# Two sequence layers on one core: the Hadamard transform of W2 moved from TensorE to VectorE and GpSimd, head states in 32 columns, first loads on three queues

## The chip, the core and the metric

One core of a Trainium2 chip runs one program. The metric is the device time of one execution in microseconds (us), as the median of several runs. The engines are TensorE (PE; its weight loads are listed as PEld), VectorE (DVE), ScalarE (ACT), GpSimd (POOL) and SyncE (SP, which here only issues DMAs). All arithmetic is float32.

## What is computed

Two layers act on 2 sequences of 1024 tokens with 512 features; each layer is a mixing part and a feed-forward part, each followed by an addition and a layer norm.

```
layer 0: x = norm(x + lightning_attention(x))      16 heads of 32, chunks of 128 tokens,
                                                   a state of 32x32 per head, decayed per chunk
         x = norm(x + fwht(silu(x W1) * (x W3)) W2) hidden size 2048, fwht = Hadamard / sqrt(2048)
layer 1: x = norm(x + selective_scan(x))           512 channels x 32 states, one step per token
         x = norm(x + (silu(x Wg) * (x Wu)) Wd)    hidden size 2048
```

The Hadamard transform acts on the hidden vector, and the matrix is symmetric. So `fwht(h) W2` equals `h (H W2) / sqrt(2048)`: the kernel transforms the 2048 rows of W2 once and keeps the result `w2h` in HBM, instead of transforming every token.

## The kernel before, in words

**Order of the work.** The kernel has a list scheduler of its own (class `Order`). Each operation is an `Op` with an engine, an estimated duration, the buffers that it reads and writes, and a priority. `Order.run` takes, again and again, the operation that can begin first by these estimates (then the lower priority number), and so writes out one fixed order for each engine. On the chip each engine works through its list in that order and waits where an operand isn't ready. The estimates (`mm_us`, `dve`, `act`, `pool`, `dma` and single numbers in the code) therefore decide the order, and nothing else. `dma` estimates a queue of its own of 220 GB/s for each issuing engine.

**Groups and phases.** The 2048 tokens are five groups of 2, 4, 4, 4 and 2 chunks of 128 tokens. Group g passes the phases V (values of the attention), A (attention), F (feed-forward of layer 0), then the scan of layer 1, then f (feed-forward of layer 1; for groups 1 and 2 the f of the group before runs in halves, a and b). The phases of later groups and the f phases fill PE while DVE, ACT and POOL work on a scan.

**Weights.** `load_weights` brings 256 KB pieces through a ring of 12 buffers, in the order of use, all on SP's queue. The pieces of the second matrix of F come from `w2h` and wait until all of it is stored.

**First loads** (`load_first`): on SP the identity, x of group 0 (2 chunks), one constant, x of group 1 (4 chunks), then Wv, two quarters of W2, Wq, Wk, two more quarters of W2, and the small constants.

**W2** (`transformed_w2`, `butterflies` L1152, `w2_products` L1171): four quarters of 128 of its 512 columns. In a quarter, row 128 c + p lies in partition p at place c (tile 128 x 16 x 128). DVE does the 4 butterfly steps over c (two operations of 1024 columns each, two tiles `w2f` and `w2b` taking turns). PE multiplies by a 128 x 128 Hadamard matrix (4 products of 512 columns a quarter) for the steps over p, ACT scales by 1/sqrt(2048) from PSUM (L1178), and SP stores the quarter.

**Attention blocks** (`attention`, `block`): a block has four heads (128 features) and four slots of 128 tokens. PE transposes the keys (L717), DVE multiplies by key decays (`kd`, L724), PE forms the state updates, one 128x128 product for each chunk (L780) of which only the four 32x32 diagonal blocks are wanted; DVE masks them with `blk` (L788) and chains them over the chunks (L796, L798) into `own` and `last`. PE forms scores (L828), DVE multiplies them by the decay mask (L846), PE adds the state's part (L872, 128x128) and the scores' part (L880) in one bank, DVE gates (L899), and a norm over each head follows (PE L916, ACT, DVE L931). Decayed queries `qd` are made by DVE for group 0, by POOL for the others (L736).

**Scan** (class `Scan`): for each of 32 states POOL multiplies `du` by B (L1375), ACT makes exp(delta a) (L1395), DVE scans (L1423) and multiplies by C (L1436), POOL (L1472) and an accumulating DMA on POOL's queue sum the products. The tile `da` of the scans lies in PSUM; `dbu`, `du`, B and C lie in SBUF. The softplus of `delta` ends with an addition of two SBUF tiles on DVE (L1307). PE transposes the sums `y` (L1501).

Of the kernel before, what the change touches and what calls it, by code (L numbers as in the profile page):

```python
# [16 lines left out]
P = 128  # L17
# [184 lines left out]
def two_layers(  # L202
# [25 lines left out]
    Pools = type("Pools", (), {"sb": None, "w2": 0, "w": 0})  # L228
# [14 lines left out]
    tagged("own", 2, lambda: wk1, [P, CG - 1, P])  # L243
    tagged("last", 3, lambda: ap_, [P, EB, P])
# [4 lines left out]
    tagged("w2f", 4, lambda: tw, [P, FC, D // 4])  # L249
    tagged("w2b", 3, lambda: tw, [P, FC, D // 4])  # L250
# [18 lines left out]
    def mm_us(n, cols):  # L269
        return n * max(cols * 4 / 2400 + 0.006, 0.28 if cols <= P else 0)  # L270
# [4 lines left out]
    def dve(cols, fn, **kw):  # L275
        return Op("DVE", 0.145 + cols * 1.05e-3, fn, **kw)
# [4 lines left out]
    def pool(cols, fn, **kw):  # L281
        return Op("POOL", 0.15 + cols * 2.25e-3, fn, **kw)
# [12 lines left out]
    w2h_b = [Buf() for _ in range(4)]  # L295
# [50 lines left out]
    def load_weights():  # L346
        for i, (src, b, needs) in enumerate(pieces):
            if i in (EB, 3 * EB):
                Pools.w = i
                yield lambda: Pools.w2 >= i // EB // 3 * 2 + 2  # L350
            yield dma(
                KB256, lambda: b.t if len(src.shape) == 2 else b.t.rearrange(
                    "p (k c) -> p k c", k=2
                ), lambda: src, a=[("w", b)], r=needs,
            )
# [22 lines left out]
    def load_others():  # L378
        for gi in range(1, len(GROUPS)):
            yield gate_before(max(PHASES.index(f"V{gi}") - 1, 0))  # L380
            yield from load_x(gi)
# [15 lines left out]
    early = tw.tile([P, 4, P], F32, name="early", bufs=1)  # L397
# [8 lines left out]
    ident_b, consts_b, decays_b, scan_b, early_b, hadamard_b = (Buf() for _ in range(6))  # L406

    def load_first():
# [3 lines left out]
        yield dma(KB256 / 4, lambda: ident, lambda: consts[:, C_ID : C_ID + P], w=[ident_b])  # L412
        yield from load_x(0)
        yield dma(
            65536, lambda: early[:, 0, :], lambda: consts[:, C_H : C_H + P], w=[hadamard_b]
        )
        spawn(load_weights())
        spawn(transformed_w2())
        spawn(load_consts())

    def load_consts():
# [8 lines left out]
        for j, c0 in ((1, C_DIFF), (2, C_MASK), (3, C_IDX)):  # L430
            yield dma(
                65536, lambda: early[:, j, :], lambda: consts[:, c0 : c0 + P],
                w=[early_b] if j == 3 else [],
            )
# [15 lines left out]
        def decays():  # L450
            nc.scalar.activation(kd_dec, ldb, AF.Exp, scale=rev)
            nc.scalar.activation(ch_dec, ldp, AF.Exp, scale=float(P))
            for k in range(EB):
                nc.scalar.activation(
                    q_dec[:, k, :], early[:, 3, :], AF.Exp, scale=ldp[:, k : k + 1]
# [76 lines left out]
    def normalized(gi, c, stage, store=None):  # L532
# [22 lines left out]
        yield Op("DVE", 0.95, moments, w=[xb, s], prio=urgent)  # L555
# [14 lines left out]

# [42 lines left out]
    def attention(gi, nxt, prio):  # L613
# [65 lines left out]
        def head_decays():  # L679
# [3 lines left out]
            for eb in range(EB):  # L683
                b = dms[eb]

                def made():
                    for j in range(HPB):
                        h = eb * HPB + j
                        nc.scalar.activation(
                            b.t[:, at_slot(j)], early[:, 1, :], AF.Exp, scale=ldb[:, h : h + 1]  # L690
                        )

                def masked():
                    d = b.t.rearrange("p (j c) -> p j c", c=P)
                    nc.vector.tensor_mul(
                        d, d, early[:, 2, :].unsqueeze(1).to_broadcast([P, HPB, P])
# [12 lines left out]
        def block(vb):  # L709
# [67 lines left out]
            def updates():  # L777
                for s, eb in enumerate(blocks(vb)):
                    for c in range(m):
                        nc.tensor.matmul(  # L780
                            bank2.t[:, at_slot(s * m + c)],
                            kd.t.rearrange("p (c s e) -> p c s e", c=n, s=S)[:, c, s, :],
                            v2[c].t[:, eb * P : (eb + 1) * P], start=True, stop=True,
                        )

            def chain():
                u = bank2.t[:, : S * m * P].rearrange("p (c e) -> p c e", e=P)
                nc.vector.tensor_mul(u, u, blk.unsqueeze(1).to_broadcast([P, S * m, P]))  # L788
# [14 lines left out]
            def chained():  # L803
                a = [("own", own)]
                if left is not None and vb == 0:
                    a.append(("last", left))
                yield Op(
                    "DVE", 0.7 + 0.34 * S * m, chain, r=[bank2] + ([] if first else [came]),
# [58 lines left out]
            def outputs():  # L867
                opening = True
                for q, (s, c) in enumerate(slots):
                    if first and c == 0:  # L870
                        continue
                    nc.tensor.matmul(  # L872
                        bank3.t[:, at_slot(q)], into[vb * S + s][c], qd.t[:, at_slot(q)],
                        start=opening, stop=False, skip_group_check=True,
                    )
# [37 lines left out]
            def norm():  # L913
# [15 lines left out]
                def scaled():  # L929
# [7 lines left out]
                    "DVE", 0.2 * S + 0.55, scaled, r=[sg, oT.whole], w=[parts[vb]], free=[sg]  # L937
# [76 lines left out]
    def ffn(ph, xT, store, prio=0):  # L1014
# [5 lines left out]
        for fh, nt in enumerate(parts):  # L1020
# [84 lines left out]
            def down(c, last):  # L1105
                bank, xb = accs[c], xn[gi, xT.cs[c]]

                def add():
                    nc.vector.tensor_add(xb.t, bank.t, xb.t)  # L1109
# [18 lines left out]

    q_d = D // 4

    def transformed_w2():
        for dq in range(4):
            f, b = Buf(), Buf()
            cols = slice(dq * q_d, (dq + 1) * q_d)
            if dq == 2:
                yield lambda: Pools.w >= 3 * EB
            yield dma(
                4 * KB256, lambda: f.t, lambda: w2t[:, cols].rearrange("(c p) d -> p c d", p=P),
                a=[("w2f", f)],
            )  # L1140
            Pools.w2 += 1
            spawn(butterflies(dq, f, b), 0.5)
            spawn(w2_products(dq, f, b), -0.3)

    def butterflies(dq, f, b):
        eng = nc.vector
        src, dst = f, b
        for i, s in enumerate((1, 2, 4, 8)):
            def half(fn, k):
                a = src.t.rearrange("p (g two s) d -> p g two s d", two=2, s=s)  # L1150
                o = dst.t.rearrange("p (g two s) d -> p g two s d", two=2, s=s)
                fn(o[:, :, k], a[:, :, 0], a[:, :, 1])  # L1152

            yield dve(
                1024, lambda: half(eng.tensor_add, 0), r=[src],
                w=[] if i == 0 else [dst], a=[("w2b", b)] if i == 0 else [],
            )
            yield dve(1024, lambda: half(eng.tensor_sub, 1), r=[src], w=[dst])
            src, dst = dst, src
        ready[dq].written = order.free["DVE"]  # L1160

    ready = [Buf() for _ in range(4)]

    def w2_products(dq, f, b):

        cols = slice(dq * q_d, (dq + 1) * q_d)
        for c4 in range(4):
            bank = Buf()
            s4 = slice(c4 * 4, (c4 + 1) * 4)
            yield pe(  # L1170
                mm_us(1, 512), lambda: nc.tensor.matmul(  # L1171
                    bank.t, early[:, 0, :], f.t[:, s4, :].rearrange("p c d -> p (c d)"),
                    start=True, stop=True,
                ),
                r=[ready[dq], f, hadamard_b], a=[("mm", bank)], free=[f] if c4 == 3 else [],
            )
            yield act(
                512, lambda: nc.scalar.mul(  # L1178
                    b.t[:, s4, :].rearrange("p c d -> p (c d)"), bank.t, 1.0 / math.sqrt(FF)
                ),  # L1180
                r=[bank], w=[b], free=[bank],
            )
        yield dma(
            4 * KB256, lambda: w2h[:, cols].rearrange("(c p) d -> p c d", p=P), lambda: b.t,
            r=[b], w=[w2h_b[dq]], free=[b],
        )
# [9 lines left out]
    class Scan:  # L1196
# [83 lines left out]
        def softplus(self, k, bank, u):  # L1280
# [11 lines left out]
            def logs():  # L1292
# [14 lines left out]
                T, lambda: nc.vector.tensor_add(r.t[:, :T], a.t[:, :T], r.t[:, :T]),  # L1307
# [78 lines left out]
        def decays(self):  # L1386
# [3 lines left out]
            for i, (n, k0) in enumerate(self.units):  # L1390
                da, delta = self.da[i], self.delta[k0 // self.W]
                for j in range(self.W):
                    def exp():
# [6 lines left out]
                    yield act(  # L1400
                        self.T, exp, r=[delta, scan_b] + ([da] if j else []),
# [241 lines left out]
```

## Time and profile before

| | |
|---|---|
| three runs | 1854.38, 1857.88, 1861.66 us; median 1857.88 |
| the profiled execution | 1856.51 us, its span on the core 1854.7 us, 19906 instructions |
| mean granted clock of PE | 0.983 of full speed |
| PE products of F and f, first matrices (L1036) | 2936 records, 900 us busy |
| PE products of F and f, second matrices (L1090) | 1024 records, 449 us busy |
| DVE scans (L1423) | 640 operations, 672 us |
| POOL products and sums of the scan (L1375, L1472) | 379 operations, 972 us |
| DMA | 336 MB, mean 181 GB/s |

A float32 product appears as two matmul records on PE. A row of the groups reads: line, engine, operation, output <- inputs, shape, count | busy us, mean ns of one | idle time of the engine just before, and what ended it. A row of a timeline reads: start, duration, engine, line, operation, count, and in brackets the idle time before it with what ended it. The granted clock is the share of PE's full speed that the chip allowed in a stretch.

### The profile page before, as it was taken

The page shows a single profiled execution, that of the slowest core. Times are in us where ns is not written, and L with a number is a line of the kernel's source. Part 1 is how long each engine was busy: PE and PEld are TensorE (multiplying, and loading weights), DVE is VectorE, ACT ScalarE, POOL GpSimd, SP SyncE. Part 2 cuts the span into 40 slices and gives each one's busy share as a digit, 9 for nine tenths or more (in the row PEclk, how much of TensorE's full clock was granted, in tenths as well). Part 3 has the DMA queues.
Part 4 walks back from the last instruction along what each step waited for, and adds up shares of the span by engine and source line. Part 5 has one row for each costly group of instructions (what it writes and reads, how often), then busy time and mean ns, then how long its engine had stood idle before and what let it go on. Part 6 is the DMA issues. An engine that isn't in the chain of part 4 may idle for free.

```text
span 1854.7 us, 19906 instructions
## 1 busy us (share of the span) xinstructions
PE 1786.2 (96%) x6392; PEld 1020.5 (55%) x6392; DVE 1327.2 (72%) x1573; ACT 1147.7 (62%) x1819; POOL 1069.5 (58%) x558
## 2 busy tenths in 40 slices
PE   7999999999979999999899999999999998999998
PEld 4547755444555744444667444577775344544574
DVE  6432136996499999943899999639999898998211
ACT  3543057697757785766576758666776857775221
POOL 0000016884467898922778889527899877786000
PEclk9999999999989999999899999999999999999999
DMA  9504445674546988835378878467999675676252
GB/s 262 178 29 142 147 131 156 182 198 141 183 126 191 258 215 227 217 106 161 110 198 262 210 203 245 119 225 218 268 279 250 186 200 170 177 187 164 74 170 86
DMA packets 227704, 336.25 MB, mean 181 GB/s; under 512 B 21264, under 2 KB 131216, under 8 KB 227600
## 3 DMA queue, kind: packets, MB, share of 16 engines
q1 hardware_dynamic: 209024, 271.53, 45.7%
q0 software_dynamic: 16272, 59.25, 17.3%
q10 hardware_dynamic: 2304, 4.20, 0.6%
q8 instruction: 51, 0.84, 0.2%
q14 instruction: 53, 0.43, 0.1%
HBM read 253.12 MB, written 22.54 MB: 149 GB/s over the span
## 4 chain that ended last, share of the span: by engine, by line
PE 67%; DVE 18%; ACT 9%; issue 5%; DMA 2%; SPq 0%; DVEq 0%; ACTq 0%
PE mm L1036 32%; PE mm L1090 18%; DVE da L1423 10%; PE mm L646 5%; DVE dbu L1436 3%; PE mm L595 3%; ACT da L1395 2%; ACT L488 2%; ACT L1395 2%; PE mm L981 1%; PE mm L828 1%; PE mm L514 1%; PE mm L880 1%; PE mm L1171 1%; DMA C<-rows 1%
## 5 line engine op out<-in xcount | busy, mean ns | idle before, releaser
L1375 POOL TENSOR_TENSOR dbu<-du,B 128x1024 f32<-128x1024 f32 x256 | 648.2, 2547 | 147.7 <-DMA y<-dbu 107.4
L1036 PE MATMUL mm<-xT,w 128*128 128x512 f32 (+1 forms) x1912 | 669.4, 511 | 1.1 <-DMA w<-in_w3t_dram 0.5
L1036 PEld LDWEIGHTS mm<-xT,w 128*128 128x128 f32 x1912 | 364.4, 191 | 305.0 <-issue 268.7
L1395 ACT ACTIVATE da<-delta,a_s 128x512 f32<-128x512 f32 (+1 forms) x640 | 384.4, 605 | 152.0 <-DVE dbu L1436 124.5
L1423 DVE TENSOR_TENSOR_SCAN da<-da,hlast,dbu 128x512 f32<-128x512 f32 (+1 forms) x384 | 425.8, 1109 | 35.1 <-ACT da L1395 23.6
L1472 POOL TENSOR_TENSOR y<-y,dbu 128x1024 f32<-128x1024 f32 x123 | 324.0, 2634 | 54.7 <-DVE dbu L1436 50.7
L1090 PE MATMUL mm<-w,h 128*128 128x512 f32 x768 | 337.2, 595 | 3.9 <-DVE h L1067 3.6
L1436 DVE TENSOR_TENSOR dbu<-da,C 128x1024 f32<-128x1024 f32 x256 | 313.0, 1223 | 13.3 <-ACT hlast L1448 6.4
L1423 DVE TENSOR_TENSOR_SCAN da<-da,dbu 128x256 f32<-128x256 f32 (+1 forms) x256 | 245.8, 960 | 12.6 <-ACT da L1395 5.7
L1090 PEld LDWEIGHTS mm<-w,h 128*128 128x128 f32 x768 | 145.2, 191 | 177.3 <-issue 167.8
L1036 PE MATMUL mm<-xf,w 128*128 128x256 f32 x1024 | 230.7, 384 | 4.2 <-ACT hf L488 2.3
L1036 PEld LDWEIGHTS mm<-xf,w 128*128 128x128 f32 x1024 | 195.2, 192 | 39.7 <-issue 4.7
L488 ACT ACT_TABLE_LOAD x141 | 180.9, 1283 | 7.8 <-PE mm L1036 2.9
L488 ACT ACTIVATE h<-mm 128x512 f32<-128x512 f32 x144 | 85.7, 597 | 134.4 <-PE mm L1036 66.2
L1395 ACT ACT_TABLE_LOAD x106 | 136.0, 1283 | 1.9
L1067 DVE TENSOR_TENSOR h<-h,mm 128x512 f32<-128x512 f32 x96 | 65.3, 681 | 93.6 <-PE mm L1036 88.5
L736 POOL TENSOR_TENSOR qd<-h,q_dec 128x512 f32<-128x512 f32 x14 | 17.9, 1276 | 190.0 <-PE mm L872 167.5
L646 PE MATMUL mm<-xT,w 128*128 128x512 f32 (+1 forms) x320 | 118.3, 518 | 5.7 <-DVE sc L846 3.9
L1448 ACT COPY hlast<-da 128x2 f32<-128x2 f32 (+1 forms) x160 | 25.3, 158 | 155.9 <-DVE dbu L1436 134.1
L1109 DVE TENSOR_TENSOR xn<-mm,xn 128x512 f32<-128x512 f32 x60 | 41.0, 684 | 104.3 <-PE mm L1090 104.0
L288 POOL DMA_DIRECT2D y<-dbu x113 | 108.7, 962 | 8.1 <-DVE dbu L1436 3.2
L1090 PE MATMUL mm<-w,hf 128*128 128x512 f32 x256 | 112.1, 592 | 0.0
(96 smaller groups left out, 1393.9 us busy)
## 6 DMA issues: line engine op xcount, KB each, us to landing
y<-dbu POOLq DMA_DIRECT2D x113, 512.0 KB, 6.1
w<-in_wgut_dram SPq DMA_DIRECT2D x192, 256.0 KB, 4.3
B<-rows SPq DMA_DIRECT2D x128, 256.0 KB, 4.6
C<-rows SPq DMA_DIRECT2D x128, 256.0 KB, 4.3
w<-in_wdnt_dram SPq DMA_DIRECT2D x96, 256.0 KB, 4.8
w<-in_w1t_dram SPq DMA_DIRECT2D x80, 256.0 KB, 3.9
w<-in_w3t_dram SPq DMA_DIRECT2D x80, 256.0 KB, 4.6
w<-w2h SPq DMA_DIRECT2D x80, 256.0 KB, 4.4
```

The costliest lines, as they stand in the source:

```text
L288: return Op(eng, us, lambda: of.dma_start(dst(), src(), **more), dma=nbytes, **kw)
L488: nc.scalar.activation(dst, src, AF.Silu)
L595: nc.tensor.matmul(bank.t, xT.t[:, k, c * P : (c + 1) * P], w_v[k].t, start=k == 0, stop=k == EB - 1,)
L646: nc.tensor.matmul(bank.t[:, s * T : (s + 1) * T], w_qk[j][k].t[:, eb * P : (eb + 1) * P], xT.t[:, k, :], start=k == 0, stop=k == EB - 1,)
L1036: nc.tensor.matmul(bank.t[:, s * T + c0 * P : s * T + c1 * P], blocks[fb // 2][j][k // 2].t[:, k % 2 * 2 * P + k0 : k % 2 * 2 * P + k0 + P ...
L1067: 512, lambda: nc.vector.tensor_mul(t.t, t.t, pu.t), r=[pu], w=[t], free=[pu]
L1090: nc.tensor.matmul(accs[c].t, hT[f // S].t[:, s * T + c * P : s * T + (c + 1) * P], w_d[f].t, start=f == 0, stop=f == nt * S - 1,)
L1375: 1024, lambda: nc.gpsimd.tensor_mul(self.wide(self.db[i]), self.wide(du), self.row(self.bs, i)),
L1395: nc.scalar.activation(d[:, j, :], self.wide(delta)[:, j, :], AF.Exp, scale=a_s[:, k0 + j, n : n + 1],)
L1423: nc.vector.tensor_tensor_scan(d()[:, j, :], d()[:, j, :], self.wide(db)[:, j, :], init, ALU.mult, ALU.add,)
L1436: 1024, lambda: nc.vector.tensor_mul(self.wide(db), d(), self.row(self.cs, i)),
L1472: 1024, lambda: nc.gpsimd.tensor_add(y.t, y.t, db[i].t), r=o, w=[y],
```

## The change

**W2.** It is cut into four blocks of 512 rows. In a block, 32-row strip m and row i of it lie at place m of partition 32 g + i, where g is the quarter of the columns: a tile of 128 x 16 x 128 whose rows of 512 bytes come by four loads of 256 KB, one for each g, on POOL's queue. Steps 1, 2, 4, 8 over m are butterflies in 128-column runs. Then DVE transposes every 32 x 32 block of the tile (two operations of 1024 columns), so that the row within a strip becomes a column, and steps 1 to 16 over it are butterflies too; then it transposes back. For blocks 0 and 2 those five steps (10 operations each) run on POOL. Two more steps (`across`, 16 operations) add and subtract whole blocks. Sixteen stores of 256 KB on SP end it. There is one tag of seven tiles (`w2`) for all of this. The PE products, the ACT evictions and the Hadamard constant go; the factor 1/sqrt(2048) moves into the addition after F's second product (`down`, one DVE operation as before).

**Head states.** The updates are now one product for each head: 128 rows by 32 columns, 32 columns moving, into the 32 partitions of the head. `own` and `last` have 32 columns, the mask is gone, and the chain works on 32 columns. The state's part of the output is four products of 32 rows by 32 columns for each slot.

**First loads.** The identity goes through ACT's queue, W2 through POOL's; SP begins with x of group 0 and goes on with Wv, Wq and Wk, and only then x of group 1 and the constants.

**Estimates.** PE, DVE and POOL operations get new estimates, with single ones for layer norm, head norm, softplus, decays, scans and the end of the sums (6 to 14 us).

```diff
-    tagged("own", 2, lambda: wk1, [P, CG - 1, P])
-    tagged("last", 3, lambda: ap_, [P, EB, P])
+    tagged("own", 2, lambda: wk1, [P, CG - 1, HD])
+    tagged("last", 3, lambda: ap_, [P, EB, HD])
...
-        return n * max(cols * 4 / 2400 + 0.006, 0.28 if cols <= P else 0)
+        return n * max(cols * 1.68e-3 + 0.012, 0.28 if cols <= P else 0)
...
-        return Op("DVE", 0.145 + cols * 1.05e-3, fn, **kw)
+        return Op("DVE", 0.075 + cols * 1.05e-3, fn, **kw)
...
-        return Op("POOL", 0.15 + cols * 2.25e-3, fn, **kw)
+        return Op("POOL", 0.2 + cols * 2.3e-3, fn, **kw)
...
+                        for j in range(HPB):
+                            e0 = j * HD
+                            nc.tensor.matmul(
+                                bank2.t[e0 : e0 + HD, (s * m + c) * HD : (s * m + c + 1) * HD],
+                                kd.t.rearrange("p (c s e) -> p c s e", c=n, s=S)[
+                                    :, c, s, e0 : e0 + HD
+                                ],
+                                v2[c].t[:, eb * P + e0 : eb * P + e0 + HD],
+                                start=True, stop=True,
+                            )
...
-                u = bank2.t[:, : S * m * P].rearrange("p (c e) -> p c e", e=P)
-                nc.vector.tensor_mul(u, u, blk.unsqueeze(1).to_broadcast([P, S * m, P]))
+                u = bank2.t[:, : S * m * HD].rearrange("p (c e) -> p c e", e=HD)
...
+                    for j in range(HPB):
+                        rows = slice(j * HD, (j + 1) * HD)
+                        nc.tensor.matmul(
+                            bank3.t[rows, at_slot(q)], into[vb * S + s][c][rows, :],
+                            qd.t[rows, at_slot(q)],
+                            start=opening, stop=False, skip_group_check=True,
+                        )
...
+        todo = [butterfly(s, q_d) for s in (1, 2, 4, 8)] + [turned]
+        todo += [butterfly(s, 1) for s in (1, 2, 4, 8, 16)] + [turned]
+
+        def within(k):
+
+            src, dst = loaded[k], Buf()
+            for i, fn in enumerate(todo):
+                slow = k % 2 == 0 and 5 <= i < 10
+                yield from step(src, dst, fn, i == 0, i == len(todo) - 1, slow)
+                src, dst = dst, src
+            halves[k] = src
...
-            self.summed.written = max(y.written for y in ys) + 6.0
+            self.summed.written = max(y.written for y in ys) + 14.0
```

In the lists of instructions, PE goes from 3390 to 3710 products (16 fewer of 512 columns; 56 updates and 56 outputs become 224 each), DVE from 1575 to 1611 operations and POOL from 563 to 599. After the first 360 us PE's list differs from the one before in single places only; `y`'s transposes for group 3 stand four products later.

## The prediction

> **What bounds the kernel now.** I read the page first (busy times, then the chain), then the busy time in stretches of 25 us, then the groups by line and shape, and last the timelines of single engines where a step needed a price.
>
> ```profile
> PE 1786.2 (96%) x6392; PEld 1020.5 (55%) x6392; DVE 1327.2 (72%) x1573; ACT 1147.7 (62%) x1819; POOL 1069.5 (58%) x558
> PE 67%; DVE 18%; ACT 9%; issue 5%; DMA 2%; SPq 0%; DVEq 0%; ACTq 0%
> ```
>
> TensorE (PE) is busy in 1786 of 1855 us and holds two thirds of the chain: the time is PE's work plus PE's gaps (68.5 us). Stretches (length, then busy PE, PEld, DVE, ACT, POOL, granted clock, DMA, GB/s):
>
> ```profile
> 0.00:25.00 25.00, 16.84 (x45) 9.12 (x46) 9.64 (x12) 5.53 (x7) 0.20 (x4) 1.00 0.98 298
> 25.00:50.00 25.00, 20.55 (x70) 11.39 (x69) 21.08 (x21) 12.26 (x28) 0.00 (x0) 0.86 0.86 222
> 50.00:75.00 25.00, 23.39 (x147) 15.21 (x146) 19.44 (x33) 16.38 (x28) 0.00 (x0) 1.00 0.61 191
> 75.00:100.00 25.00, 23.71 (x71) 10.31 (x69) 1.42 (x4) 9.09 (x15) 0.00 (x0) 0.93 0.35 105
> 1100.00:1125.00 25.00, 25.00 (x60) 11.13 (x59) 24.10 (x23) 19.20 (x28) 21.66 (x13) 1.00 0.88 243
> ```
>
> In the scans (last row) PE is full beside a full VectorE (DVE): a us taken from PE's work is a us of the end, since PE still has some 140 us to do after the last scan (from 1710 to 1850). In the first 75 us PE has gaps of 14 us, and after gaps the clock drops (0.86). The transform of W2 lies there, and there POOL is idle. The groups:
>
> ```profile
> L1171 PE MATMUL mm<-w2f,early 128*128 128x512 f32 x32 | 18.8, 704 | 4.4 <-DVE w2f L1152 3.1 <-ACT w2b L1178 1.3
> L1152 DVE TENSOR_TENSOR w2b<-w2f 128x1024 f32<-128x1024 f32 x16 | 18.9, 1220 | 14.6 <-DMA w2f<-in_w2t_dram 14.5
> L780 PE MATMUL mm<-h,kd 128*128 128x128 f32 x112 | 15.4, 277 | 1.6 <-DVE kd L724 1.6
> ```
>
> **Part 1, W2 off PE.** Sixteen 512-column products go (two records each): 18.8 us of PE, and the 4.4 us that it waited for them, 23 us. Their 16 evictions (9.4 us of ACT) go too; ACT is busy in 17.8 of the first 50 us there, so that is worth nothing while PE has work; if ACT were late, it would be worth up to 9 us more. This is the whole direct gain.
>
> **Part 2, W2 onto DVE and POOL.** Before, DVE did 32 additions of 1024 columns; now it does 52 butterflies, 16 sums across and 16 block transposes, and POOL does 20 butterflies. Additions run at 1.17 us each back to back (two in 2.36 us in DVE's timeline): 68 x 1.17 = 80 us. No row has a block transpose. Below: a one-operand copy of 128 columns takes 0.289 us and a statistics pass over 512 takes 0.683, so 1024 would take 1.2; above: a scan's 1.225 us for 512, so 2.45. I take 1.2, the nearer in kind: 16 x 1.2 = 19 us; the upper end adds 20. The Trainium skill (VectorE: DVE Perf Modes, The three transpose paths) has 311 ns for 128x128 in bf16; eight of those would be 2.5 us, an estimate, and 40 us for the sixteen; no run shows it.
>
> Attention's own DVE work up to the last sum, in the changed program's list at the durations of before: 28 score products for 13 us, 24 chain steps for 7, 34 others for 20: 40 us. So DVE has 80 + 19 + 40 = 139 us in one in-order queue, where before it had some 80 busy up to 175 us.
>
> *The hidden cost is between POOL and DVE.* DVE's timeline, then POOL's (start, duration, both times):
>
> ```profile
> 488.54 2.58 DVE L1307 TENSOR_TENSOR pt<-th,pt 128x512 f32<-128x512 f32 x1 [0.74 <-ACT pt L1298]
> 541.83 1.94 DVE L931 SCALAR_TENSOR_TENSOR xT<-xT,nw,sg 128x512 f32<-128x512 f32 x1
> ```
> ```profile
> 488.22 2.35 POOL L1375 TENSOR_TENSOR dbu<-du,B 128x1024 f32<-128x1024 f32 x1 [4.46 <-DMA du<-dd]
> 540.87 2.35 POOL L1472 TENSOR_TENSOR y<-y,dbu 128x1024 f32<-128x1024 f32 x1 [2.58 <-DVE dbu L1436]
> ```
>
> L1307 takes 0.69 us elsewhere, and here it ends 0.55 us after POOL's operation ends (490.57); L931 does the same (543.22). Both have two operands in SBUF. L1436, with one operand in PSUM, doesn't mind POOL:
>
> ```profile
> L1436 DVE TENSOR_TENSOR dbu<-da,C x256: 1207/1225/1227, 293.5 to 1707.1; 128x1024 f32<-128x1024 f32 x128
> ```
>
> Butterflies have both operands in SBUF, on both engines, so I let them exclude each other. The Trainium skill (SBUF — State Buffer, Who interferes with whom) says such a pair blocks fully, which speaks against sharing this work out: by the rule taken for every operation POOL's 47 us would all be lost to DVE's additions; going by L1436 alone, nothing.
>
> The sum by rows: POOL's first ten (23.5 us) start when the first 11 DVE operations are done, near 22 us; DVE then waits for dm until about 33, so most of them are free: 4 us lost. The second ten, with two qd products, are 26 us; the stretch of DVE between its release and its need of POOL's result has 29 us, 17 of them with two SBUF operands; 17 + 26 = 43, so 14 us lost. Together 18; bounds 0 and 47.
>
> DVE's clock, then. It starts on W2 near 9 us (a queue of its own; before, at 15.45 behind x and Wv), does 13 us, and meets dm, which needs the constants: landed at 38.6 before, behind 8.6 MB on SP's queue; now 4.5 MB are ahead of them there, but the 4 MB of W2 compete; I take dm ready at 33 (30 to 40). Then 126 us are left, 18 lost to POOL, 5 of waits: the last sum at 182. Then three quarters of W2 must be stored (3 MB at 250 to 300 GB/s and a landing, about 12) and loaded again (4.4): F0's first down product at 199. Before, it ran at 188.8, with its rows in place since 87 us: that cover of 90 us is used up.
>
> ```profile
> 188.78 13.90 PE L1090 MATMUL mm<-w,hf 128*128 128x512 f32 x32
> 359.13 55.10 PE L1036 MATMUL mm<-xT,w 128*128 128x512 f32 x128
> ```
>
> The landmark is F1's second run of 64 products (359.13). From F0's down product to it the new list has 150 us of PE work (88 products of 256 columns at 0.44, 122 of 512 at 0.86, some 6 for the rest), 4 of waits as before: 353; 2 us for clock lost in gaps: **355, 4 earlier**. If PE set this stage, it would be 359 - 23 = 336.
>
> **Part 3, states in 32 columns.** Updates: 56 products of 0.22 us become 224. Nearest is L880, also 128 rows by 32 columns: 16 in 1.01 us, 0.063 each, so 14.1 against 12.5; a quarter of that if columns counted, 3.5. Inter-chunk outputs: 56 of 0.22 become 224 of 32 by 32; by L880 14.1, by L828 (16 in 1.84 us) 25.8. I take L880 twice, +3, of which 2 lie after the landmark; bounds -9 and +15. A page of the Trainium skill (TensorEngine Tiling (Array Packing), Key Properties) says that a change of tile shape drains PE; no row separates that. On DVE each block loses its mask (0.69 us) and 96 columns of four operations: 1.1 us each.
>
> **Part 4, queues and estimates.** x of group 1 goes behind Wq and Wk on SP, so Wv comes sooner, against W2's loads on POOL: 0 (bounds -4, +4). POOL's 16 issues cost 0.96 us each by the y accumulation; at most 3.5 if they scale with the pieces moved (512 rows of 512 bytes, against 144 packets for each of the 113 y accumulations), and then W2 starts later by up to 10 us. SP issues 16 stores of W2 in place of 4 and of the 4 loads; its issues of 0.3 to 0.5 us lie beside PE's 150 us and cost nothing unless the ring of weights runs dry, which the 17 us after the last sum already hold. Scaling by 1/sqrt(2048) moves into an addition that keeps 0.684 us (L899's form): 0. After the landmark PE's list is nearly the same. Two waits there shrink: y's transposes come 4 products later (a wait of 3.7 us and half-speed clock behind it): -4; the chains of A2 to A4 (PE waited 2.66 and 1.91 us for them, then ran at half speed): -4. Gaps and clock lost after the landmark are 43 + 20 us, so this term lies between -25 and, if the new order opens gaps, +12.
>
> **Sum:** -4 + 2 - 8 = -10 on the profiled execution's 1856.5 us (span 1854.7), which is 1.4 below the median 1857.9: **1847 us**.
>
> **Rivals.** *PE keeps its gain* (collisions cheap, as L1436 says): landmark 336, so -23 + 2 - 8 = -29, 1828. For: POOL's work could fall beside scores and chains, which read PSUM. Against: L1307 and L931. *Slower: POOL locks DVE out.* All 47 us of POOL's butterflies fall on DVE's, 29 more than I count: +19, 1876. It passes zero where the loss exceeds 18 + 10 = 28 us. For: DVE's queue is in order, and F0's down product waits for its last sum. *It doesn't do what it says:* the gain at the landmark is given back since DVE is full in the scans (24.1 of 25 us): 1855. Against: DVE idles between the scans (5.6 of 25 us at 450 to 475), PE doesn't.
>
> **Numbers.** Forecast case 45 in 100 (1835 to 1862; 25 of it below 1848.6), PE keeps its gain 22, slower 28, given back 5. Half a per cent, 9.3 us, is about what a measurement of this kernel can tell from no change. Faster 25 + 22 = 47; same 20 + 5 = 25; slower 28. The range takes in the rivals' cores: 1822 to 1880.
>
> **What would show it.** PE without L1171, at about 1770 us of busy time; DVE butterflies of over 2 us exactly where POOL has one; POOL's butterflies in two runs, from about 22 and about 100 us; the last sum near 182 and F0's first down product near 199; the landmark near 355. Wrong if butterflies stay at 1.22 us beside POOL (then 1828), if transposes take over 2 us, or if the stretches after the landmark gain or lose over 15 us.

## The result, and the profile after

The changed kernel takes 1879.69 us (median of four, 1877.96 to 1883.89), the kernel before beside it 1857.06: 1.0126 times as long, with a 95% interval of 1.0099 to 1.0154. It is slower by 22.6 us; I had forecast 10 faster. The execution shown took 1879.03 us, its span 1877.3, the mean granted clock of PE fell from 0.983 to 0.975.

Page of the changed kernel, busy times and chain:

```profile
PE 1782.3 (95%) x7032; PEld 1010.0 (54%) x7032; DVE 1392.3 (74%) x1609; ACT 1146.0 (61%) x1808; POOL 1137.6 (61%) x594
PE 53%; DVE 21%; ACT 9%; DMA 8%; issue 5%; POOL 4%; SPq 0%; DVEq 0%; POOLq 0%; ACTq 0%
```

PE's share of the chain falls from 67 to 53%. PE idles 95.0 us (68.5 before), and its busy time falls by 3.9 us only, though L1171 (18.8) is gone and the updates are 8.6 cheaper (L780 15.4, now L779 6.8). So some 23 us of busy time are the same work taking longer. Some 15 of them go with the lower clock (an estimate: 1877.3 us at 0.975 lose 46.9 us, 1854.7 us at 0.983 lose 31.5); what the other 8 are isn't shown.

Stretches of the changed kernel (length, then busy PE, PEld, DVE, ACT, POOL, granted clock, DMA share, GB/s):

```profile
25.00:50.00 25.00, 18.89 (x128) 14.67 (x127) 18.83 (x10) 10.81 (x24) 22.72 (x14) 0.86 0.89 243
50.00:75.00 25.00, 18.57 (x145) 11.16 (x146) 23.18 (x36) 12.38 (x22) 6.87 (x4) 0.80 0.35 103
125.00:150.00 25.00, 20.56 (x190) 11.05 (x186) 24.79 (x22) 6.90 (x9) 18.41 (x7) 0.93 0.36 121
450.00:475.00 25.00, 18.46 (x48) 8.27 (x47) 19.46 (x29) 19.95 (x38) 17.06 (x10) 0.98 0.80 229
1100.00:1125.00 25.00, 25.00 (x59) 11.02 (x58) 24.62 (x23) 11.05 (x20) 23.23 (x13) 1.00 0.76 207
```

In the first three rows DVE or POOL is full and PE has gaps at a low clock: DVE sets the start now. The fourth row is a gap that no new instruction stands near; before, PE was full in these 25 us:

```profile
450.00:475.00 25.00, 25.00 (x76) 11.71 (x74) 5.58 (x13) 18.92 (x32) 4.40 (x4) 1.00 0.37 121
```

Groups of the changed kernel by line and shape:

```profile
L1191 DVE TENSOR_TENSOR w<-w 128x1024 f32<-128x1024 f32 x52 | 81.7, 1605 | 14.2 <-DMA w<-in_w2t_dram 14.0
L1191 POOL TENSOR_TENSOR w<-w 128x1024 f32<-128x1024 f32 x20 | 54.1, 2715 | 34.2 <-DVE w L1197 33.5
L1219 DVE TENSOR_TENSOR w<-w,w 128x1024 f32<-128x1024 f32 x16 | 22.0, 1422 | 0.0
L1197 DVE STREAM_TRANSPOSE w<-w 128x1024 f32<-128x1024 f32 x16 | 19.3, 1226 | 0.1
L779 PE MATMUL mm<-h,kd 128*32 128x32 f32 x448 | 6.8, 199 | 1.8 <-DVE kd L720 1.6 <-ACT xT L518 0.2
```

A transpose takes 1.226 us (I took 1.2; the 2.5 us that the prediction gives beside it is twice too much). DVE's butterflies average 1.605 us in place of 1.22. POOL's average 2.715; two that ran while DVE was idle (from 27.95 to 34.12) took 1.94 each, so the prediction's 2.35, a scan's multiplication, was too long for them. The engines delay each other. DVE's timeline, then POOL's (start, duration):

```profile
34.73 3.08 DVE L1191 TENSOR_TENSOR w<-w 128x1024 f32<-128x1024 f32 x1
37.73 2.84 DVE L732 TENSOR_TENSOR qd<-h,q_dec 128x512 f32<-128x512 f32 x1
40.49 0.68 DVE L720 TENSOR_TENSOR kd<-mm,kd_dec 128x512 f32<-128x512 f32 x1
41.09 3.12 DVE L691 TENSOR_TENSOR dm<-dm,early 128x512 f32<-128x512 f32 x1
44.13 9.93 DVE L1191 TENSOR_TENSOR w<-w 128x1024 f32<-128x1024 f32 x3
```
```profile
30.32 3.88 POOL L1191 TENSOR_TENSOR w<-w 128x1024 f32<-128x1024 f32 x2
...
34.80 5.21 POOL L1191 TENSOR_TENSOR w<-w 128x1024 f32<-128x1024 f32 x2
...
41.27 5.13 POOL L1191 TENSOR_TENSOR w<-w 128x1024 f32<-128x1024 f32 x2
...
47.01 5.97 POOL L1191 TENSOR_TENSOR w<-w 128x1024 f32<-128x1024 f32 x2
```

qd (L732) takes 2.84 us on DVE in place of 0.65, the mask (L691) 3.12 in place of 0.69, three butterflies 9.93 in place of 3.5. kd (L720), which reads PSUM, keeps 0.68, but it fell between two of POOL's butterflies. That operations with a PSUM operand aren't held up is seen later, where four score products (L847) and kd run beside POOL at 0.62 and 0.67 us (DVE, then POOL):

```profile
116.84 2.47 DVE L847 TENSOR_TENSOR sc<-mm,dm 128x512 f32<-128x512 f32 x4
119.24 0.67 DVE L720 TENSOR_TENSOR kd<-mm,kd_dec 128x512 f32<-128x512 f32 x1
```
```profile
115.92 4.60 POOL L1191 TENSOR_TENSOR w<-w 128x1024 f32<-128x1024 f32 x2
```

PE's timeline shows what the long operations do:

```profile
54.88 2.07 PE L829 MATMUL mm<-h 32*128 32x128 f32 x14 [5.28 <-DVE last L799]
58.50 1.08 PE L713 MATMUL mm<-cst,h 128*128 128x128 f32 x4 [1.55 <-DVE sc L847]
59.38 5.99 PE L591 MATMUL mm<-w,xT 128*128 128x512 f32 x8
...
74.69 3.60 PE L591 MATMUL mm<-w,xT 128*128 128x512 f32 x8
...
216.23 3.60 PE L1094 MATMUL mm<-w,hf 128*128 128x512 f32 x8
...
365.41 55.10 PE L1040 MATMUL mm<-xT,w 128*128 128x512 f32 x128
```

PE waits 5.28 us for `last`, whose small DVE operations stand behind those three butterflies. Then eight records of L591 take 5.99 us in place of 3.60. F0's first down product is at 216.23, the landmark at 365.41: 6.3 later than before (359.13). The other 16.3 us come after the landmark: 1511.9 us from there to the end, 1495.6 before. All 16 lie between the landmark and the start of F2's second run of 64 products. Before, the changed kernel, and two kernels of the experiments below, 12 and 8 (length, busy PE, PEld, DVE, ACT, POOL, clock, DMA, GB/s):

```profile
359.13:728.65 369.52, 356.60 (x1297) 199.52 (x1296) 311.92 (x361) 268.58 (x437) 271.12 (x140) 0.98 0.68 190
365.41:750.99 385.58, 360.40 (x1490) 196.68 (x1488) 325.17 (x385) 284.33 (x469) 293.24 (x153) 0.97 0.70 191
347.56:717.24 369.68, 356.83 (x1297) 199.59 (x1296) 311.48 (x361) 268.58 (x437) 271.26 (x141) 0.98 0.70 191
358.83:744.93 386.10, 360.97 (x1490) 197.33 (x1488) 323.85 (x385) 284.14 (x468) 292.30 (x152) 0.97 0.69 190
```

### The profile page after: what moved, and what is told of

Same layout as the page of the kernel before. It is cut to its first block, busy times and chain, and to the rows that moved or that the text cites. A ratio compares the mean times of both kernels' runs of the same rounds, so it can differ in the third digit from the quotient of the medians.

```text
span 1877.3 us, 21292 instructions
## 1 busy us (share of the span) xinstructions
PE 1782.3 (95%) x7032; PEld 1010.0 (54%) x7032; DVE 1392.3 (74%) x1609; ACT 1146.0 (61%) x1808; POOL 1137.6 (61%) x594
## 4 chain that ended last, share of the span: by engine, by line
PE 53%; DVE 21%; ACT 9%; DMA 8%; issue 5%; POOL 4%; SPq 0%; DVEq 0%; POOLq 0%; ACTq 0%
PE mm L1040 28%; PE mm L1094 15%; DVE da L1484 9%; DMA y<-dbu 4%; DVE dbu L1497 4%; DVE w L1191 3%; PE mm L642 3%; POOL dbu L1436 2%; ACT da L1456 2%; PE mm L591 2%; ACT L1456 1%; ACT L485 1%; POOL y L1533 1%; PE mm L985 1%; DMA w<-in_wq_dram 1%
## 5 line engine op out<-in xcount | busy, mean ns | idle before, releaser
L1040 PEld LDWEIGHTS mm<-xT,w 128*128 128x128 f32 x1912 | 363.4, 191 | 304.0 <-issue 270.5
L1533 POOL TENSOR_TENSOR y<-y,dbu 128x1024 f32<-128x1024 f32 x123 | 319.1, 2594 | 55.5 <-DVE dbu L1497 47.3
L1094 PE MATMUL mm<-w,h 128*128 128x512 f32 x768 | 341.3, 600 | 5.2 <-DMA w<-w2h 2.1
L1497 DVE TENSOR_TENSOR dbu<-da,C 128x1024 f32<-128x1024 f32 x256 | 312.8, 1222 | 11.1 <-ACT hlast L1509 4.2
L1330 POOL TENSOR_TENSOR xn<-xn,dp 128x512 f32<-128x512 f32 x16 | 22.7, 1421 | 165.4 <-PE mm L511 152.9
L642 PEld LDWEIGHTS mm<-xT,w 128*128 128x128 f32 x320 | 61.8, 200 | 57.8 <-issue 42.5
```

The costliest lines, as they stand in the source:

```text
L642: nc.tensor.matmul(bank.t[:, s * T : (s + 1) * T], w_qk[j][k].t[:, eb * P : (eb + 1) * P], xT.t[:, k, :], start=k == 0, stop=k == EB - 1,)
L1040: nc.tensor.matmul(bank.t[:, s * T + c0 * P : s * T + c1 * P], blocks[fb // 2][j][k // 2].t[:, k % 2 * 2 * P + k0 : k % 2 * 2 * P + k0 + P ...
L1094: nc.tensor.matmul(accs[c].t, hT[f // S].t[:, s * T + c * P : s * T + (c + 1) * P], w_d[f].t, start=f == 0, stop=f == nt * S - 1,)
L1497: 1024, lambda: nc.vector.tensor_mul(self.wide(db), d(), self.row(self.cs, i)),
L1533: 1024, lambda: nc.gpsimd.tensor_add(y.t, y.t, db[i].t), r=o, w=[y],
```

## Experiments

Theories: **A**, the W2 transform costs what is lost, by POOL locking DVE out, by its loads, or since its products on PE had cost little; **B**, the new estimates gave a worse list; **C**, the list past the start is a deal: any edit of costs or operations reorders it, and the time moves by chance. "Landmark" is the start of F1's second run of 64 products, "rest" the span from there to the end, both of the profiled execution.

| kernel | median, us | before beside it | ratio (95%) | landmark | rest |
|---|---|---|---|---|---|
| before | 1857.1 | | | 359.1 | 1495.6 |
| changed | 1879.7 | 1857.1 | 1.0126 (1.0099-1.0154) | 365.4 | 1511.9 |
| 1 estimates alone | 1869.4 | 1855.9 | 1.0073 (1.0049-1.0097) | 353.4 | 1512.7 |
| 2 states alone | 1853.8 | 1855.9 | 0.9983 (0.9968-0.9998) | 347.3 | 1503.6 |
| 3 states and estimates | 1858.7 | 1857.1 | 1.0017 (1.0004-1.0031) | 342.7 | 1518.9 |
| 4 W2 and queues alone | 1878.1 | 1855.9 | 1.0118 (1.0096-1.0140) | 360.8 | 1517.6 |
| 5 changed, old estimates | 1880.0 | 1857.1 | 1.0126 (1.0107-1.0145) | 359.2 | 1520.3 |
| 6 changed, 6 us after sums | 1888.7 | 1857.1 | 1.0174 (1.0155-1.0192) | 362.8 | 1524.5 |
| 7 changed, POOL's part left out | 1861.7 | 1855.9 | 1.0031 (1.0018-1.0044) | 351.6 | 1512.1 |
| 8 all on DVE | 1872.8 | 1857.1 | 1.0090 (1.0069-1.0111) | 358.8 | 1512.7 |
| 9 all on DVE, half the loads on SP | 1862.0 | 1859.4 | 1.0019 (1.0006-1.0032) | 348.8 | 1515.3 |
| 10 changed, half the loads on SP | 1877.8 | 1857.9 | 1.0112 (1.0087-1.0138) | 362.2 | 1511.8 |
| 11 as 9, old estimates | 1878.8 | 1857.9 | 1.0113 (1.0086-1.0139) | 359.8 | 1519.8 |
| 12 before without W2's products | 1845.2 | 1859.4 | 0.9922 (0.9899-0.9944) | 347.6 | 1499.2 |
| 13 before, ACT cost 0.20 for 0.18 | 1870.3 | 1859.4 | 1.0060 (1.0043-1.0076) | 358.4 | 1509.6 |
| 14 before, ACT cost 0.16 | 1864.8 | 1857.9 | 1.0043 (1.0024-1.0063) | 349.8 | 1513.1 |
| 15 before, DVE cost 0.165 for 0.145 | 1846.5 | 1857.9 | 0.9939 (0.9915-0.9962) | 345.9 | 1495.7 |
| 16 changed, ACT cost 0.20 | 1883.8 | 1859.4 | 1.0127 (1.0109-1.0146) | 365.2 | 1517.6 |
| 17 states alone, DVE cost 0.165 | 1861.2 | 1857.4 | 1.0023 (1.0006-1.0039) | 342.9 | 1518.8 |
| 18 as 9, DVE cost 0.095 for 0.075 | 1866.3 | 1857.4 | 1.0048 (1.0035-1.0062) | 344.8 | 1517.8 |

**The parts alone (1 to 5).** 1 takes over the new estimates, 2 the states, 3 both; 4 is the changed kernel with states and estimates of before, 5 the changed kernel with the old estimates.

> The kernel before with the new estimates alone (the planner's costs and the 14 us in place of 6 after the sums); W2, states and queues as before. Theory 1, the planner's new list opened the gaps between the two landmarks of F1 and F2 (365.41 to 750.99, 16 us longer than before): these 16 us come back here, 1873. Theory 2, the late W2 pushed everything behind it and the list only followed: within 5 us of before, 1852 to 1862. What I forecast for the estimates, -8: 1849.

> The kernel before with the head states in 32 columns alone. The changed kernel's rows say PE works 8.6 us less in the updates (15.4 to 6.8) and 0.4 more in the inter-chunk products, so -8 where PE sets the end: 1849. The rival, shapes that change drain PE and the price lies outside of the records: 1857 or more. The forecast's +3: 1860.

> The kernel before with states in 32 columns and the new estimates; only W2 and its queues as before. If the parts add up (+13.5 and -2): 1867. If the estimates fit the new states, near 1853. Against the changed kernel's 1879.7 this tells what W2's transform costs in its own company: 13 if parts add up, 27 if not.

> The changed kernel with the states and the estimates of before: W2 on DVE and POOL and the three queues stand alone. Theory 1 (the list's gaps come from the estimates): only the loss of the start is left, 6 us and the 8 that the states no longer save, 1871 less 16, so 1863 or so is the price of W2 alone. Theory 2 (W2 being late is the whole loss): 1880 or more, since the states' 8 us are given up as well.

> The changed kernel with all estimates of before: W2's transform, the queues and the states. If the parts add up, W2 alone (+22) and the states (-2 to -4): 1876. If the new estimates are needed for the new list, it is slower than W2 alone, over 1880. If the estimates are a loss here as they are on the kernel before (+13.5), the changed kernel gets that back: 1866.

The estimates alone cost 13.5 us, as B says; but with the changed W2 and states they cost nothing (5: 1880.0, changed: 1879.7). So they aren't worse in themselves. W2 alone costs 22, as A says, and against a kernel with the same states and estimates (3) the changed one loses 21.0 at the end and 22.7 at the landmark. With the states alone (2) the landmark comes 11.8 earlier and the end 2; kernel 15 below has its landmark 13.2 earlier with no change of work at all, so the 11.8 aren't shown to be the states' own.

**POOL's share and the loads (7 to 10).**

```diff
-                slow = k % 2 == 0 and 5 <= i < 10
+                slow = False
...
+            if k == 2:
+                yield lambda: Pools.w >= 3 * EB
...
-                    eng="POOL", a=[] if g else [("w2", f)], w=[f] if g else [],
+                    eng="POOL" if k < 2 else "SP", a=[] if g else [("w2", f)], w=[f] if g else [],
```

The first pair is 8, the other lines are 10, both together are 9. In 7 the steps for which `slow` holds are skipped.

> The changed kernel with POOL's twenty butterflies left out (the rows of W2 in two of four parts miss five of their ten steps), nothing in their place: DVE keeps all that it has. If the lock between POOL and DVE is what cost the start, DVE's two-operand work gains about 28 us (what its instructions take over their own length beside POOL), PE's waits for DVE there (about 17 us) go, and the landmark of F1 comes near 345, 20 earlier; the end by 10 to 20, 1860 to 1870. If the long queue of DVE alone cost it, landmark and end move by under 5.

> The changed kernel with all 72 butterflies on DVE and none on POOL. If POOL and DVE exclude each other, POOL's help was worth nothing: DVE takes on 20 x 1.17 = 23.4 us and loses the 28.6 that its operations took over their own length beside POOL, so the landmark of F1 comes 0 to 5 earlier and the end is 1872 to 1880. If the two ran side by side, DVE's queue grows by 23 us and the end by 15 to 23, 1895 to 1903.

> The changed kernel with all butterflies on DVE, and the second half of W2's loads behind Wq and Wk on SP's queue in place of POOL's. With all of W2 early on POOL's queue (the run with all on DVE alone), PE waited 13 us for Wv, Wq, Wk and wg in its first 45 us. If the two queues share one stream from memory, these waits shrink to 6 or so and the landmark of F1 comes 5 to 8 earlier, the end at 1865 to 1868; if the waits come from elsewhere, 1873 again.

> The changed kernel with one move: the second half of W2's loads behind Wq and Wk on SP's queue, not early on POOL's. POOL keeps its twenty butterflies. Against the run that has this move and all butterflies on DVE (1862.0) it tells what POOL's share costs with the transfers settled. If POOL and DVE exclude each other: the same time or up to 8 more, 1862 to 1870. If POOL's help is worth its 23 us once the transfers are settled: 1845 or so.

DVE's butterflies with none on POOL (8, group by line):

```profile
L1191 DVE TENSOR_TENSOR w<-w 128x1024 f32<-128x1024 f32 x72 | 86.2, 1231 | 13.8 <-DMA w<-in_w2t_dram 13.5
```

72 butterflies take 86.2 us where 52 took 81.7: taking 20 off DVE saved 4.5 us of butterflies. Its other operations lost more than that. DVE's busy time up to the landmark is the third number of these rows, for 8 and for the changed kernel (length, PE, PEld, DVE, ACT, POOL):

```profile
0.00:358.83 358.83, 323.82 (x1604) 189.66 (x1605) 218.15 (x290) 137.21 (x235) 59.70 (x48) 0.96 0.49 140
0.00:365.41 365.41, 327.77 (x1605) 192.75 (x1606) 224.75 (x270) 137.42 (x235) 113.72 (x68) 0.94 0.48 138
```

With POOL's help DVE is busy 6.6 us longer, with 20 operations fewer, and the landmark comes 6.6 later, the end 6.9. With the loads settled (10 against 9) POOL's help costs 13.4 us at the landmark and 15.8 at the end, more than either case had. Leaving POOL's part out (7, loads as in 8 and the changed kernel) brings the landmark 13.8 earlier than in the changed kernel (20 if the lock cost the start) and the end 18.0; against 8 the end is 11.1 earlier. These comparisons are free of theory C: behind the landmark the traces of the changed kernel and of 7 to 10 have the same operations in the same order on PE, DVE, ACT and POOL, and their rests are 1511.8 to 1515.3. The loads: what PE waited for in the first 62 us, with all on DVE (8), then with half the loads on SP (9) (us in total, times, longest):

```profile
PE mm L591 <- DMA w<-in_wv_dram: 5.5, 4, 2.0
PE mm L642 <- DMA w<-in_wq_dram: 4.8, 2, 2.5
...
PE mm L661 <- DMA wg<-in_wg_dram: 2.8, 1, 2.8
```
```profile
PE mm L591 <- DMA w<-in_wv_dram: 4.7, 4, 2.4
...
PE mm L661 <- DMA wg<-in_wg_dram: 1.6, 1, 1.6
```

The wait for Wq goes; the landmark comes 10.0 earlier, the end 10.9. In the changed kernel the same move is worth 3.2 and 1.9 only: there POOL's queue holds seven of the sixteen issues back behind its own butterflies (until 56.23), and PE has no wait for Wq in its first 62 us. With the move PE's wait for `last` grows from 5.3 to 10.0 us.

**W2's products on PE (12).** The PE products and ACT evictions of before are left out and the quarter is stored as DVE leaves it.

> The kernel before without the sixteen products of W2 on PE and their evictions, nothing in their place (W2 misses the 128-wide part of its transform); DVE's 32 additions, loads and stores stay. If my step was right that the 23 us of L1171 lie on the path: the landmark of F1 (359.13 before) comes at 336 and the end at 1833 to 1840. If these products only filled PE's waits for the first weights and for attention's own chains: the landmark comes less than 8 earlier, the end within 6 of before, 1851 to 1861.

Between the two cases: 11.6 at the landmark, 14.2 at the end. PE's timeline before, then without the products:

```profile
32.96 8.41 PE L1171 MATMUL mm<-w2f,early 128*128 128x512 f32 x12 [3.13 <-DVE w2f L1152]
41.30 0.64 PE L665 MATMUL mm<-xT,wg 128*32 128x256 f32 x8
```
```profile
29.04 0.66 PE L717 MATMUL mm<-cst,h 128*128 128x128 f32 x4 [0.69 <-ACT h L488]
36.99 1.08 PE L665 MATMUL mm<-xT,wg 128*32 128x256 f32 x8 [7.29 <-DMA wg<-in_wg_dram]
```

The gate product L665 needs `wg`, and without W2's products PE waits 7.29 us for it, until 36.99. Before, W2's records stood in that hole. The 11.6 us aren't a clean price of the products, though: kernel 12 keeps the order of before behind the landmark (rest 1499.2 and 1495.6), but not in the start, and 14 and 15 below have their landmarks 9.3 and 13.2 earlier with all the products in place.

**One estimate by a hair (6, 13 to 16).** 6 sets the 14 us after the sums back to 6; in the others one number of `act` or `dve` moves by 0.02 us:

```diff
-        return Op("ACT", 0.18 + cols * 0.81e-3, fn, **kw)
+        return Op("ACT", 0.2 + cols * 0.81e-3, fn, **kw)
```

> The changed kernel with one estimate of before: 6 us, not 14, between the last sum of a scan and its outputs. If the y transposes that now come at 508.75 and not at 455.05 are what empties PE between the landmarks of F1 and F2 (25.0 us idle there, 12.9 before), 12 us come back: 1867. If the cause is in the other estimates or in the whole order, under 5 either way: 1875 to 1885.

> The kernel before with one estimate moved by a hair: 0.20 in place of 0.18 us in the planner's cost of an ACT operation. No instruction is added or removed; from the list's middle on the order differs in some hundred places. If the order past the start is dealt by chance, the end moves by 5 to 15 us either way; if the planner's order is stable in value, by under 3.

> The kernel before with 0.16 in place of 0.18 us in the planner's cost of an ACT operation: a second hair's breadth, the other way. Dealt by chance: away from before by over 4 us, on either side; if 0.20 was slower by 11 because it is the wrong side of the truth, this one is the same or faster.

> The kernel before with 0.165 in place of 0.145 us in the planner's cost of a DVE operation: a third hair's breadth. Dealt by chance, and before a lucky deal: slower by 4 to 15. Otherwise within 3.

> The changed kernel with the same hair's breadth (0.20 for 0.18 us of an ACT operation). Few orders move here. Dealt by chance: 1870 to 1890, away from 1879.7 by more than 3; stable: within 3 of it.

No operation changes, and the kernel before becomes 0.6% slower, 0.4% slower or 0.6% faster. Both directions of the ACT number are slower, so it isn't that one side is nearer the truth. C holds: the order is a deal with a spread of some 24 us, and the rest of before, 1495.6, is the shortest in the table. The start is dealt as well: the lists of 13 are those of before up to the landmark, and it comes 0.8 earlier; those of 14 and 15 part from them within the first 55 us, and it comes 9.3 and 13.2 earlier. A deal belongs to the list and not to the run: kernels with the same order behind the landmark have nearly the same rest (before and 12; 5 and 11; the changed kernel and 7 to 10). Kernel 6 lies outside both cases of its expectation.

**Deals of other kernels (11, 17, 18).**

> The changed kernel with all butterflies on DVE, half of W2's loads on SP, and the estimates of before. If the later part of the list is dealt by chance, not by the estimates' quality, the landmark of F1 stays near 403 on the scale on which it is 413 before and 419 in the changed kernel, and the end is anywhere from 1852 to 1872. If the new estimates were a loss in themselves (13.5 on the kernel before): 1850.

> The kernel before with states in 32 columns and with 0.165 in place of 0.145 us in the planner's cost of a DVE operation: the two edits that were faster, together. If they add up: 1846.5 less 2 to 4, 1843. If the order is dealt anew with each edit: anywhere in 1845 to 1870, the span of the other deals of the kernel with W2 on PE.

> The changed kernel with all butterflies on DVE, half of W2's loads on SP, and 0.095 in place of 0.075 us in the planner's cost of a DVE operation. If W2 on DVE costs some 11 us beside W2 on PE whatever the deal (the three so far: 1862.0, 1872.8, 1878.8; with W2 on PE 1846.5 to 1870.3): 1860 to 1880. If 1862.0 was only an unlucky deal and this one is good: under 1855.

The old estimates cost 16.8 us on 9, where on the kernel before the new ones cost 13.5. In 11 the landmark was to stay, and it comes 11.0 later than in 9: here too the start is dealt. The two edits that were faster alone (2 and 15) are slower together. So a single pair of kernels with different lists tells the price of an edit only to some 10 us; the deals taken together tell more:

| W2's transform | kernels | median times | mean | landmark, mean | rest, mean |
|---|---|---|---|---|---|
| PE and DVE (before, 1-3, 13-15, 17) | 8 | 1846.5 to 1870.3 | 1860.2 | 349.9 | 1508.5 |
| DVE alone (8, 9, 11, 18) | 4 | 1862.0 to 1878.8 | 1870.0 | 353.1 | 1516.4 |
| DVE and POOL (changed, 4-6, 10, 16) | 6 | 1877.8 to 1888.7 | 1881.3 | 362.6 | 1517.3 |

The first and the last row overlap neither in their times nor in their landmarks (342.7 to 359.1, and 359.2 to 365.4). Over these deals the transform on DVE and POOL costs some 21 us on average, 13 of it in the start. The deals aren't all independent: 8, 9, 10 and the changed kernel share one order behind the landmark, 16 nearly has it, and 5 and 11 share another.

## Why the prediction was wrong

**"L1171 off PE: 23 us."** At most half shows in kernel 12: 11.6 at the landmark, and a new deal of the start alone can give that much (13.2 in 15). Part of the remainder is a wait that L1171 filled, and that `wg` (7.29 us) now fills. I read "PE has gaps of 14 us in the first 75" and still charged every PE product there at full price.

**"18 us lost to POOL, bounds 0 and 47."** I counted 28.6 by DVE's instructions beside POOL over their own length: 14.2 in the second ten (I had 14), 14.4 in the first ten, where I had 4. I let POOL start at 22 and run while DVE waited for the constants until 33. POOL started at 26.93, its queue also issued loads between butterflies, and it ended at 56. `dm` came at 34.12, as forecast, so seven of POOL's first ten butterflies fell on a busy DVE. The mechanism was right, the size not; the rival that named it (1876) had the price of 28 us at which the gain is used up.

**DVE's clock.** W2 started at 14.89 (9 forecast: its loads took longer), the last sum ended at 190.5 (182), F0's first down product came at 216.23 (199), since the sixteen stores went out until 203.4. Not all of this reached the end: the planner had put the second layer norm's and F's products ahead. The landmark came 6.3 later, not 4 earlier: 10.4 of the miss.

**"After the landmark PE's list is nearly the same: -8."** This is the step that failed most: the rest is 16.3 us longer, outside my bounds of -25 and +12 on that term, and 22.3 of the 32.6 us between forecast and result. (The sum took its 10 us off the profiled execution; off the median, 1857.9, it is 1848.) The two waits that I named did go: PE doesn't wait for `last` in A2 (2.66 us before) nor for POOL's `y` (3.72). Others took their place. PE's timeline of the changed kernel, then of the one before, in the same us of the span:

```profile
460.90 0.66 PE L511 MATMUL mm<-cst,xn 128*128 128x128 f32 x4 [2.05 <-ACT xn L549]
...
473.35 5.40 PE L1298 MATMUL mm<-xT,wbc 128*128 128x512 f32 x8 [4.49 <-ACT xT L518]
```
```profile
455.05 1.04 PE L1501 MATMUL mm<-cst,y 128*128 128x128 f32 x8
...
459.97 3.60 PE L1237 MATMUL mm<-xT,wbc 128*128 128x512 f32 x8
```

Before, `y`'s transposes and the next products filled these us; now the transposes stand at 508.75 and PE waits for ACT. Between the landmarks of F1 and F2 PE idles 25.2 us (12.9 before). PE's list itself had this move: behind the landmark, without the products of the head states, `y`'s transposes of group 0 come 53 products later and those of group 1 12, where I had read only the four of group 3. The 14 us in place of 6 didn't place them there: in kernel 6 they come 135 us after the landmark (143 in the changed kernel, 96 before), and it is slower still. The order as a whole makes the gap: every kernel with the changed kernel's order has it (idle 24.1 to 25.3 us there in 7 to 10) whatever its start, and kernel 12 with the order of before doesn't (12.8). The order changes with a hair's breadth of one estimate, and the kernel before happens to have a good one; kernel 3, with W2 on PE and the changed kernel's states and estimates, has a rest of 1518.9, longer than the changed kernel's. So the long rest isn't shown to come from W2's move. I compared PE's list alone and took the landmark for the state of the whole program. DVE's first scans fell further behind than the landmark did (first and last start, before, then changed):

```profile
L1423 DVE TENSOR_TENSOR_SCAN da<-da,dbu x256: 683/955/1232, 286.3 to 794.3; 128x256 f32<-128x256 f32 x64, 128x512 f32<-128x512 f32 x64
L1484 DVE TENSOR_TENSOR_SCAN da<-da,dbu x256: 683/956/1232, 325.1 to 819.0; 128x256 f32<-128x256 f32 x64, 128x512 f32<-128x512 f32 x64
```

The first scan starts 38.8 us later, the landmark 6.3: PE's list had put other products ahead, and 36 scans lie before the landmark in place of 60.

**"Tiles of 32: +3."** The updates got cheaper, 15.4 to 6.8 us, inside my bounds; the outputs cost the same (L872 20.1, L875 20.5). The end shows 2 us of it in kernel 2.

**What stays open.** The kernels with W2 off PE have a rest 8 us longer on average. It holds more work: in every one of them only 36 scans lie before the landmark, in every kernel with W2 on PE 60, and in the changed kernel POOL is busy 27.7 and ACT 23.0 us longer after it than before the change. They also share the later loads of x for the next groups. Which of these is the cause, or whether it is the deal, wasn't tried. Nor is it shown what the states do: their landmark comes 11.8, 10.7 and 3.0 us earlier and their rest is 8, 6 and 23 us longer in the pairs 2 to before, 3 to 1 and 17 to 15, and new deals without any change of work move both as far.

**A faster version.** Kernel 15, before with 0.165 in place of 0.145 us for a DVE operation, beats both: 1846.5, a ratio to before of 0.9939. It is a better deal, not a better cost.

## What to carry to other kernels

Work on the busiest engine is worth its time only where that engine doesn't wait: look at what lies in the gaps beside it before you charge it to the path. Work shared between DVE and POOL with both operands in SBUF gained nothing here where both ran at once (DVE was busy 6.6 us longer), and it held up the small DVE operations behind it. A landmark on one engine tells how far that engine is: look at where the others stand too. Where a planner deals the order, measure the spread of the deals first (move an estimate by a hair, three times); a change smaller than that spread is judged by the means of several deals, not by one, or by kernels whose lists are the same behind the change.

## What the runs showed of the hardware

- A two-operand SBUF operation of DVE beside one of POOL's mostly takes 2.8 to 3.4 us in place of 0.65 to 1.22, and POOL's up to 3.4 in place of 1.94. 20 butterflies moved to POOL took 4.5 us off DVE's butterflies and left DVE busy 6.6 us longer in all (224.75 and 218.15). The Trainium skill (SBUF — State Buffer, Who interferes with whom) calls the shared pair of ports an exclusive lock; the rows agree, and the operation with a PSUM operand doesn't mind POOL here either:

```profile
L1497 DVE TENSOR_TENSOR dbu<-da,C x256: 1202/1224/1226, 329.0 to 1729.6; 128x1024 f32<-128x1024 f32 x128
```

- A float32 transpose of 32 by 32 blocks over 128x1024 takes 1.226 us on DVE: as long as an addition of that size.
- A state update as four products of 128 rows by 32 columns costs 0.12 us (6.8 us for 56), as one of 128 by 128 it cost 0.275 (15.4).
- PE's waits can cost twice, but needn't. In the changed kernel 26.5 us more idle time came with some 23 us more busy time for the same work and a mean clock of 0.975 in place of 0.983; the stretches of the start that are shown had 0.80 to 0.93, the gap at 450 us 0.98. In kernel 13, 13.8 us more idle time than before came with no more busy time (1785.6 and 1786.2 us) at a mean clock of 0.982.
